# Six-layer windowed attention: interleaved token order with one value transfer per chunk, second norm and one Newton step on ScalarE

## The chip, the cores and the metric

The kernel runs on one core of a Trainium2 chip. The metric is device time in microseconds (us): the median of three executions before the change is 3436.73 us (3434.03 to 3436.86). The engines are TensorE (PE in the profile, with its weight loads as PEld), VectorE (DVE), ScalarE (ACT), GpSimd (POOL), and SyncE (SP), which here only issues DMA transfers. "ns" is nanoseconds.

## The reference

The input x has 32 sequences of 128 tokens and 128 channels, all in float32. Two blocks follow each other.

1. A cross-attention over a context of the same size (16 heads of 8 channels, 4 key/value heads, a time bias), added to x. The change touches none of its arithmetic.
2. Six layers, each an attention and a feed-forward part. Cut to what matters:

```python
for i in range(6):
    x = attn_layer(shift_tokens(x), Wqkv[i], q_scale[i], k_scale[i], Wo[i]) + x
    x = ffn_layer(shift_tokens(x), ln_g[i], ln_b[i], W1[i], b1[i], W2[i], b2[i]) + x

# attn_layer: 16 heads of 64 channels, windows of 32 tokens
q, k, v = split(x @ Wqkv)                 # per head
q, k = l2norm(q) * q_scale, l2norm(k) * k_scale
q, k = rotary(q) * scale, rotary(k) / scale
out = local_attention(q, k, v)            # a window sees itself and the window before it
return out @ Wo
# ffn_layer: layernorm, then a * gelu(gate), then W2
```

A sequence of 128 tokens is four windows of 32. A query in window u sees the keys of windows u-1 and u, under a mask.

## The kernel before, in words

**Work and stages.** The 32 sequences are 8 groups of 4 (`GB`). After the cross-attention (the first 430 us or so) each of the 6 layers goes over the 8 groups, and each group over its 4 sequences. One sequence of one layer is called a unit here: there are 6 x 32 = 192. The feed-forward part works on a whole group at once: 48 of these.

**A unit** (`unit`, L770) works on the transposed tokens of its group, `xh` and `xl` (the high and the low part, so that three fast matmuls give a product exact enough; `split3`, L433):

- `qk` (L435 to L437, four chunks c): tokens times weights for q and k, into a PSUM bank, token on the partition. `sq` (L787, ACT) squares it, `tab` (L793, DVE) multiplies it with the rotary tables, `ss` (L816, DVE) sums the squares, `add` (L809, POOL) adds the two rotary parts.
- `newton` (L383) turns the 32 sums per token into 1/sqrt: a floor (L396, DVE), Ln and Exp (L399, L402, ACT), then one Newton step y*(1.5 - 0.5*v*y*y) in three DVE instructions (L405, L409, L415). `mul` (L834, POOL) scales the rows, `tq` (four PE transposes a chunk, L441) turns them, `evq` (L838, ACT) copies the result from PSUM to SBUF.
- `y` (PE, L435 to L437 again, four chunks): tokens times the product of value and output weights. `yt` (L851, ACT) copies a chunk to SBUF as 128 tokens x 512. The four windows u of 32 tokens are then laid beside each other, so that a 32-partition block holds one chunk: `dm` (L861), four transfers per chunk, one per window, issued by SP; 16 per unit.

```python
for u in range(4):
    S.op("dm", lambda u=u: nc.sync.dma_start(ysh[0].t[32 * c:32 * c + 32, u * 512:(u + 1) * 512],
                                             yt.t[32 * u:32 * u + 32, :]), pri, [yt], ysh, k=c)
```

- `msk` (L884, ACT) puts the mask into two PSUM banks, `sc` (L879, PE, 64 small matmuls) adds the scores, then `mx` (L892, DVE), `fold` (L893, PE, subtracts the maximum), `ex` (L895, ACT), `sm` and `rl` (L896, L897, DVE), `pl` (L898, POOL), `pt` (L900, DVE transpose in blocks of 32).
- `av` (L913, PE, 56 matmuls over two bank halves) multiplies weights with `ysh` and needs all 16 transfers of its unit.

**A group** begins with `ax` (PE transposes of the tokens, L762), `axh` (L763, ACT copy) and `axl` (L764, DVE). It ends with `ffn` (L919): residual (L921, DVE), token shift (two DMAs on SP, L752 and L753), `st`/`ag` (L927, L931, DVE), the norm's 1/sqrt with its Newton step on POOL, `xn` (L939: four DVE instructions, 128 x 128 each, subtract mean and multiply), `ptn` (transposes, L441), `xnh`/`xnl`, `gate`/`pa` (PE, L435 to L437), `gel` (L961, ACT), `um` (L969, DVE), `w2` (L980, PE), residual (L984, DVE).

**The order of the work.** A planner in the kernel (`Sched`, L79) places every operation by a list schedule: `COST` (L32) has the engine, the occupancy and the latency that it assumes for each name, `LATER` (L55) shifts an operation's priority (in units; a number after the name is the chunk), `KEEP` (L63) keeps PSUM banks free, and the buffer pools (L247 to L286) say how many of each tile there are: 5 general PSUM banks (`pj`), 2 for scores, 3 `yt`, 2 `ysh`, 4 `qT`, 10 `rt`. The result is a fixed order of instructions on each engine and on SP's queue; the chip then runs each engine's list in order, with semaphores between them. So whatever stands first in a list and waits holds up all that stands behind it.

Of the kernel before, what the change touches and what calls it, by code (L numbers as in the profile page):

```python
# [23 lines left out]
NYD = 6  # L24
NS = 2
YD = "sb"
ADD = "pool"
XN = "dve"
# [6 lines left out]
    mxs=("POOL", .26, .30), dmx=("DVE", .17, .25), dnw=("DVE", .18, .25), ln=("ACT", .2, .24), ep=("ACT", .2, .24), nw=("POOL", .31, .34),  # L35
    mul=("POOL", 1.08, 1.1), tq=("PE", .45, .70), evq=("ACT", .5, .62), evk=("ACT", .5, .62),
    y=("PE", .69, .90), yt=("ACT", .5, .62), dm=("SP", .62, 2.3), dw=("SP", .62, 3.5), dr=("SP", .62, 4.5),
# [3 lines left out]
    eps=("POOL", .22, .26), lnf=("ACT", .22, .21), epf=("ACT", .22, .21), nwf=("POOL", .3, .34), xn=("DVE", 1.05, 1.13), xn2=("POOL", 1.08, 1.1),  # L41
# [13 lines left out]
LATER = dict(y=3, xtr=0.75, ptn=1.5, fold=0.35, qk=-0.5, xsc=-1, axh=-1, evk=-0.25, ss=0.25, sc=0.25, sq=0.5, um=0.75,  # L55
    axl=-1.5, tq=1.25, xev=1.75, mul=0.75, mx=-1, evq1=-1.0, tab0=0.25, lnb=0.5, um1=-1, xpj=0.75, yt1=-1.5, rl1=0.75,
    dw=-1, gel=0.75, xn1=1, nw=-0.25, msk0=2, yt3=-1.25, ta3=0.5, pwm=-0.4, ag=0.25, tq0=1.5, pa0=-0.5, dnw=1, io=0.6,
    xnh=1.5, ep=-1.5, mx1=0.25, pt1=1.5, adda=0.9, ex1=1, gel1=0.35, dr=-0.15, ta1=1.5, msk=-1.5, adda1=2, xo=1.5,
    ta0=0.5, sm0=2.85, xsb=3, rl0=-1, mx0=-1, wve=-1.5, um0=0.25, evq2=-1.5, tq1=0.5, add3=2.1, xnl=2, gate1=0.5,
    nwf=1, xn2=0.25, add=1.5, lof=-1.5, yt2=0.5, wvp=0.75, ta=-0.5, xn=-0.5, ldw=-0.25, tq2=-0.25, res2=0.35, pt=0.25,  # L60
    xat=2)

KEEP = dict(qk=1, y=1, gate=1, pa=3, xtr=0, xpj=0, pv=1, td=1, xsc=0, wvp=2, mp=2, bip=2, sc0=0, ax=0, tq=0)  # L63
# [159 lines left out]
def body(ctx: ExitStack, tc: tile.TileContext, x, ctx_in, fside, mask_in, xWq, xWk, xWv, xWo, xtw,  # L223
         Wqkv, q_scale, k_scale, Wo, ln_g, ln_b, W1, b1, W2, b2, cst, x1d, y2d, out):
# [18 lines left out]
    def pool(name, n, shape, dt=F32, inorder=True):  # L243
        S.pool(name, [lambda d, i=i: tl(f"{name}_{i}_", shape, d or dt) for i in range(n)], inorder)
# [7 lines left out]
    if ADD == "dma":  # L252
        pool("rt", 5, [P, 1024])
    else:
        pool("rt", 10, [P, 512])
    pool("qT", 4, [P, 512])
    pool("ysh", 2, [P, 2048])
    pool("yt", 3, [P, 512], inorder=False)
# [3 lines left out]
    pool("xl", 2, [P, GB, P], F32R)  # L262
    pool("nh", 1, [P, 512], F32R)
# [38 lines left out]

    S.pool("yd", [y2d[i] for i in range(y2d.shape[0])], False)
# [79 lines left out]
    def newton(names, pri, V, src, n, floor, eps, pool_, cols):  # L383
        v, y, t = [Buf(p) for p in pool_]

        def sl(b):
            return b.t[:, 0:n]
# [16 lines left out]
        def f3():  # L404
            e.tensor_tensor(sl(t), sl(y), sl(y), op=ALU.mult)  # L405
# [18 lines left out]
        S.op(names[3], f3, pri, [y], [t])  # L424
# [182 lines left out]
    def xgroup(g):  # L607
# [66 lines left out]
        if ADD == "dma":  # L674
            two = [Buf("rt", dt=F32R), Buf("rt", dt=F32R)]
            qs = [(two[t // 2], t % 2 * 512) for t in range(4)]
        else:
            qs = [(Buf("rt", dt=F32R), 0) for t in range(4)]
# [77 lines left out]
    def lgroup(l, g, w):  # L756
        base = l * NU + g * GB
        G = {"po": Buf("po")}
        pt = Buf("pj")
        hi, lo = G["x"] = Buf("xh"), Buf("xl")  # L760
        pri = base - 1.0
        S.op("ax", lambda: tr4(pt.t, [xsg(g)[:, k] for k in range(GB)]), pri, [X[g], XS[g]], [pt], also=[hi, lo])  # L762
        S.op("axh", lambda: nc.scalar.copy(hi.t, grp(pt.t)), pri, [pt], [hi])  # L763
        S.op("axl", lambda: nc.vector.tensor_tensor(lo.t, grp(pt.t), hi.t.bitcast(F32), op=ALU.subtract), pri, [pt, hi],  # L764
             [lo])
        for j in range(GB):
            unit(l, g, j, w, G, base + j)
        ffn(l, g, w, G, base + GB - 1)

    def unit(l, g, j, w, G, pri):  # L770
# [4 lines left out]

        hs = [(Buf("rt"), Buf("t")) for _ in range(2)] if ADD == "dma" else None

        def proj(c):
            pp, sq = Buf("pj"), Buf("sq")
            rt, t = hs[c // 2] if hs else (Buf("rt"), Buf("t"))  # L780
            o = c % 2 * 512 if hs else 0
            tok = Buf(None, 0) if hs else rt
            rts.append((rt, o, tok))
# [13 lines left out]
            def ta():  # L797
                nc.vector.tensor_tensor(rt.t[:, o:o + 512].rearrange("p (h d) -> p h d", d=64),
                                        pp.t.rearrange("p (h d) -> p h d", d=64), bc(tab.t[:, c // 2, 0], 8), op=ALU.mult)

            def tb():
                nc.vector.tensor_tensor(
                    t.t[:, o:o + 512].rearrange("p (h s d) -> p h s d", s=2, d=32)[:, :, ::-1, :],
                    pp.t.rearrange("p (h s d) -> p h s d", s=2, d=32),
                    bc(tab.t[:, c // 2, 1].rearrange("p (s d) -> p s d", s=2), 8), op=ALU.mult)

# [4 lines left out]
            if hs:  # L811
                S.op("ta", ta, pri, [pp, tab], [rt], also=[t], k=c)
                S.op("ta", tb, pri, [pp, tab], [t], k=c)
            else:
                S.op("tab", tab2, pri, [pp, tab], [t], k=c)
            S.op("ss", lambda: nc.vector.tensor_reduce(ss.t[:, c * 8:(c + 1) * 8], sq.t.rearrange("p (h d) -> p h d", d=64),  # L816
                                                       axis=AX.X, op=ALU.add), pri, [sq], [ss], k=c)
            if not hs:
                S.op("add", add, pri, [t], [rt], k=c)
            elif c % 2:  # L820
                S.op("adda", lambda: nc.gpsimd.dma_start(rt.t, t.t, accum_op=ALU.add), pri, [t, rt],
                     [rt, *(x[2] for x in rts[-2:])], k=c)
# [4 lines left out]
        for c in range(4):  # L827
            def tr(c):
                (rt, o, tok), pt, d = rts[c], Buf("pj"), Buf("qT")
                qT.append(d)  # L830

                def mul():
                    rv = rt.t[:, o:o + 512].rearrange("p (h d) -> p h d", d=64)
                    nc.gpsimd.tensor_tensor(rv, rv, rn.t[:, c * 8:(c + 1) * 8].unsqueeze(2).to_broadcast([P, 8, 64]),  # L834
                                            op=ALU.mult)
                S.op("mul", mul, pri, [tok, rn], [tok], also=[rt], k=c)
                S.op("tq", lambda: tr4(pt.t, [rt.t[:, o + k * P:o + (k + 1) * P] for k in range(4)]), pri, [tok], [pt], also=[rt, d], k=c)
                S.op("evq", lambda: nc.scalar.copy(d.t, pt.t), pri, [pt], [d], k=c)  # L838
            tr(c)
# [3 lines left out]
        yds = [Buf("yd"), Buf("yd")]  # L843
        for c in range(4):
            def yy(c):
                py, yt = Buf("pj"), Buf("yt")
                mh, ml = w["m"][c]
                yd = yds[c // 2]
                S.op("y", lambda: split3(py.t, (xh.t[:, j, :], xl.t[:, j, :]), (mh.t, ml.t)), pri, [xh, xl, mh, ml], [py],
                     also=ysh, k=c)  # L850
                S.op("yt", lambda: nc.scalar.copy(yt.t, py.t), pri, [py], [yt], k=c)  # L851
                if YD == "dram":
                    S.op("dw", lambda: nc.sync.dma_start(yd.t[:, c % 2], yt.t), pri, [yt], [yd], k=c)
                    if c % 2:
                        r = slice(32 * c - 32, 32 * c + 32)
                        S.op("dr", lambda: nc.sync.dma_start(
                            ysh[0].t[r].rearrange("p (u n) -> p u n", u=4),
                            yd.t.rearrange("u c i n -> (c i) u n")), pri, [yd], ysh, k=c)
                else:
                    for u in range(4):  # L860
                        S.op("dm", lambda u=u: nc.sync.dma_start(ysh[0].t[32 * c:32 * c + 32, u * 512:(u + 1) * 512],  # L861
                                                                 yt.t[32 * u:32 * u + 32, :]), pri, [yt], ysh, k=c)
            yy(c)
# [55 lines left out]
    def ffn(l, g, w, G, pri):  # L919
# [15 lines left out]

        if XN == "dve":
            def xnf():
                for k in range(GB):
                    nc.vector.tensor_scalar(xn.t[:, k * P:(k + 1) * P], xsg(g)[:, k], mv.t[:, k, 0:1], r.t[:, k:k + 1],  # L939
                                            op0=ALU.subtract, op1=ALU.mult)  # L940
            S.op("xn", xnf, pri, [X[g], XS[g], mv, r], [xn])
        else:
            S.op("xn1", lambda: nc.gpsimd.tensor_tensor(grp(xn.t), xsg(g), mv.t[:, :, 0:1].to_broadcast([P, GB, P]),
                                                        op=ALU.subtract), pri, [X[g], XS[g], mv], [xn])
            S.op("xn2", lambda: nc.gpsimd.tensor_tensor(grp(xn.t), grp(xn.t), r.t[:, 0:GB].unsqueeze(2).to_broadcast([P, GB, P]),
                                                        op=ALU.mult), pri, [xn, r], [xn])
# [64 lines left out]
def _constants():  # L1011
# [15 lines left out]
    rot = np.concatenate([QK_SCALE * cos * scale, QK_SCALE * sin * scale * sgn, cos / scale, sin / scale * sgn], 1)  # L1027
    idn = np.eye(N)
# [37 lines left out]
```

## Time and profile before

| | before |
|---|---|
| median of three executions | 3436.73 us |
| the profiled execution | 3450.15 us |
| its span (first to last instruction) | 3448.4 us |
| granted TensorE clock, mean | 0.972 |
| `dm` issues on SP (L861) | 3072, median 589 ns, 507 to 2076 ns |
| a `dm` from issue to landing | 1.9 / 2.0 / 4.0 us (min / median / max) |
| `xn` on DVE (L939) | 192 instructions, 131 us busy |
| first Newton product on DVE (L405) | 192 instructions, 79 us busy |
| `evq` on ACT (L838) | 768 instructions, 426 us busy |

The page has six parts: busy time of each engine; the span in 40 slices; DMA queues; the chain of work that ended last (followed back from the last instruction, at each step to what released it); the costliest groups of instructions; and DMA issues with their time to landing. A busy PE is not a PE at its peak, since the ends of pipelined matmuls are modelled. The view of waits lists who was idle and what ended it; the view of a line lists its instructions, what they waited for and who waited for them; the view of windows sums busy time over stretches of the span.

### The profile page before, as it was taken

How to read it: one execution, taken by the hardware profiler on the slowest of the kernel's cores; microseconds unless marked ns; L12 is line 12 of the kernel's file. 1: busy time of each engine (PE TensorE's matmuls, PEld its weight loads, DVE VectorE, ACT ScalarE, POOL GpSimd, SP SyncE). 2: the span in 40 equal slices, each digit the busy share in tenths (PEclk: the TensorE clock that was granted, in tenths of full speed). 3: DMA queues.
4: the chain of work that ended last, by engine and by line, in shares of the span. 5: the costliest groups of instructions: out<-in, count | busy, mean ns of one | idle time of the engine just before them, and what ended most of it. 6: DMA issues, size and time to landing. Idle time of an engine off the chain costs nothing.

```text
span 3448.4 us, 118846 instructions
## 1 busy us (share of the span) xinstructions
PE 3113.7 (90%) x47887; PEld 2404.7 (70%) x47887; DVE 2917.7 (85%) x6115; ACT 2227.7 (65%) x4415; POOL 2413.6 (70%) x2470
## 2 busy tenths in 40 slices
PE   8877899898799999799999999999999999999997
PEld 5554677676576777577777777777777777777775
DVE  5556998889678998779999889998899988899984
ACT  6766666666466666566766666666666667676664
POOL 6546877677557777656777767777677777677773
PEclk9998999999899999899999999999999999999998
DMA  4200132323133333233233333332332333333332
GB/s 105 58 13 10 48 78 67 76 68 90 41 87 74 74 80 76 56 92 74 69 79 79 87 77 78 75 82 68 91 80 69 79 74 85 79 75 87 82 78 71
DMA packets 253765, 251.06 MB, mean 73 GB/s; under 512 B 127486, under 2 KB 148258, under 8 KB 253218
## 3 DMA queue, kind: packets, MB, share of 16 engines
q1 hardware_dynamic: 252786, 243.12, 28.8%
q8 instruction: 380, 6.23, 0.9%
q14 instruction: 167, 1.37, 0.1%
q10 hardware_dynamic: 432, 0.34, 0.0%
HBM read 25.24 MB, written 4.19 MB: 9 GB/s over the span
## 4 chain that ended last, share of the span: by engine, by line
PE 34%; DVE 26%; DMA 11%; SPq 11%; ACT 10%; issue 6%; POOL 2%; ACTq 0%; POOLq 0%; DVEq 0%
SPq L861 10%; PE bank__68 L913 7%; DMA xt<-xt 2%; PE bank__66 L879 2%; PE bank__64 L441 1%; PE bank__67 L879 1%; PE bank__63 L441 1%; PE bank__61 L441 1%; PE bank__65 L441 1%; PE bank__63 L435 1%; PE bank__62 L435 1%; PE bank__62 L441 1%; PE bank__65 L435 1%; PE bank__61 L435 1%; PE bank__63 L436 1%
## 5 line engine op out<-in xcount | busy, mean ns | idle before, releaser
L884 ACT COPY bank__66<-mask 128x512 f32<-128x512 f32 x192 | 117.0, 610 | 5.7 <-PE bank__66 L362 4.4
L884 ACT COPY bank__67<-mask 128x512 f32<-128x512 f32 x192 | 116.5, 607 | 1.5 <-PE bank__67 L362 1.1
L724 ACT ACTIVATE ysh__88<-ysh__88 128x512 f32<-128x512 f32 x96 | 60.7, 634 | 57.0 <-POOL ysh__88 L722 56.9
L961 ACT ACT_TABLE_LOAD x48 | 61.6, 1283 | 0.9
L241 ACT ACT_TABLE_LOAD x48 | 61.6, 1283 | 0.9
L921 DVE TENSOR_TENSOR xt<-bank__68,xt 128x512 f32<-128x512 f32 x48 | 33.0, 687 | 16.7 <-PE bank__68 L913 16.5
L441 PE MATMUL bank__61<-cs,ysh__88 128*128 128x128 f32 x84 | 15.5, 315 | 10.2 <-ACT ysh__88 L724 10.2
L441 PE MATMUL bank__63<-cs,ysh__88 128*128 128x128 f32 x80 | 14.6, 312 | 10.8 <-ACT ysh__88 L724 10.5
L441 PEld LDWEIGHTS bank__63<-cs,ysh__88 128*128 128x128 f32 x80 | 9.9, 156 | 15.0 <-ACT ysh__88 L724 12.8
L441 PEld LDWEIGHTS bank__61<-cs,ysh__88 128*128 128x128 f32 x84 | 10.9, 160 | 13.6 <-ACT ysh__88 L724 12.2
L441 PE MATMUL bank__62<-cs,ysh__88 128*128 128x128 f32 x76 | 14.5, 324 | 5.6 <-ACT ysh__88 L724 5.4
L441 PE MATMUL bank__64<-cs,ysh__88 128*128 128x128 f32 x68 | 12.7, 318 | 7.6 <-ACT ysh__88 L724 7.5
L441 PE MATMUL bank__65<-cs,ysh__88 128*128 128x128 f32 x76 | 13.3, 302 | 6.4 <-ACT ysh__88 L724 6.1
L441 PEld LDWEIGHTS bank__62<-cs,ysh__88 128*128 128x128 f32 x76 | 10.7, 168 | 8.4 <-ACT ysh__88 L724 7.6
L695 DVE TENSOR_TENSOR xt<-bank__68,xt 128x512 f32<-128x512 f32 x8 | 5.5, 685 | 12.8 <-PE bank__68 L693 12.8
L441 PEld LDWEIGHTS bank__64<-cs,ysh__88 128*128 128x128 f32 x68 | 8.6, 159 | 10.9 <-ACT ysh__88 L724 10.2
L441 PEld LDWEIGHTS bank__65<-cs,ysh__88 128*128 128x128 f32 x76 | 9.5, 154 | 9.5 <-ACT ysh__88 L724 8.7
L991 POOL TENSOR_TENSOR raw__50988<-raw__50988,xt 128x512 f32<-128x512 f32 x1 | 1.3, 1262 | 19.7 <-DVE xt L984 19.7
L718 DVE CUSTOM_DVE_ANT_0 ysh__88<-bank__63,rt__2156 128x128 f32<-128x128 f32 x12 | 2.8, 287 | 12.7 <-ACT S__90 L727 6.2
L727 ACT COPY ysh__88<-bank__63 128x512 f32<-128x512 f32 x20 | 11.9, 597 | 1.8 <-PE bank__63 L441 1.6
L727 ACT COPY ysh__88<-bank__61 128x512 f32<-128x512 f32 x21 | 12.3, 586 | 1.2 <-PE bank__61 L441 1.1
L718 DVE CUSTOM_DVE_ANT_0 ysh__88<-bank__61,rt__2550 128x128 f32<-128x128 f32 x12 | 2.8, 288 | 12.1 <-ACT S__90 L727 5.6
(24588 smaller groups left out, 15904.7 us busy)
## 6 DMA issues: line engine op xcount, KB each, us to landing
xt<-xt SPq DMA_DIRECT2D x96, 112.0 KB, 2.5
xt<-in_x SPq DMA_DIRECT2D x16, 128.0 KB, 3.2
x_scratch<-xt SPq DMA_DIRECT2D x8, 256.0 KB, 3.0
xt<-xt SPq DMA_DIRECT2D x96, 15.0 KB, 2.2
stg__750<-in_L_ffn_Wo SPq DMA_DIRECT2D x1, 512.0 KB
stg__1904<-in_L_ffn_Wo SPq DMA_DIRECT2D x1, 512.0 KB
stg__20461<-in_L_ffn_Wo SPq DMA_DIRECT2D x1, 512.0 KB
stg__28190<-in_L_ffn_Wo SPq DMA_DIRECT2D x1, 512.0 KB
```

Source lines behind the costliest of these rows:

```text
L241: S.back = lambda: nc.scalar.preload_act_table_set("natural_log_exp_and_others")
L435: nc.tensor.matmul(pt, lh, rh, start=True, stop=False)
L436: nc.tensor.matmul(pt, lh, rl, start=False, stop=False)
L441: nc.tensor.transpose(dst[:, k * P:(k + 1) * P], srcs[k], ident)
L724: S.op("xex", lambda: nc.scalar.activation(sm.t, sm.t, AF.Exp), pri, [sm], [sm], table="E")
L727: S.op("xev", lambda: nc.scalar.copy(sm.t, pt.t), pri, [pt, sm], [sm])
L861: S.op("dm", lambda u=u: nc.sync.dma_start(ysh[0].t[32 * c:32 * c + 32, u * 512:(u + 1) * 512], yt.t[32 * u:32 * u + 32, :]), pri, [yt], y ...
L879: nc.tensor.matmul(s4[a][32 * c:32 * c + 32, half, wd, lo:64], q[r, c * P + 32 * wd:c * P + 32 * wd + 32], k[r, c * P + 32 * wd - 32 + lo: ...
L884: S.op("msk", lambda b=b: nc.scalar.copy(b.t, mask), pri, (), [b], k=a)
L913: nc.tensor.matmul(po.t[32 * wd:32 * wd + 32, j * P:(j + 1) * P], p5[a][:, half, wd, blk, :], ysh[0].t[:, u * 512 + h * P:u * 512 + (h + 1 ...
L921: S.op("res", lambda: nc.vector.tensor_tensor(xv(g), hv(po.t), xv(g), op=ALU.add), pri, [po, X[g]], [X[g]])
L961: S.op("gel", lambda: nc.scalar.activation(u.t[0:n], pg.t[0:n], AF.Gelu, bias=b1c.t[0:n, 1, i:i + 1]), pri, [pg, b1c], [u], table="G", k=i)
```

## The change

Four things are changed together.

1. **Token order.** `axh` and `axl` write the transposed tokens so that token u*32 + i stands at place 4*i + u. All products (q, k and values) then come out with that token on partition 4*i + u. The rotary tables are put in the same order on the host. `evq` puts q and k back in plain order: it reads PSUM at a step of four elements and writes SBUF in a row.
2. **Values.** A chunk of 128 partitions x 512 now lies in the order of the target's 32 partitions x 2048, and one `dm` per chunk takes the place of four. `dm` has a new assumed latency (3.2 for 2.3).
3. **Second norm.** `xn` moves from DVE to ACT: four activations with scale and bias per partition. A small DVE instruction, `nmr`, first makes the bias, -mean/sqrt. `ysq` (ACT Square) takes the place of the first of the three DVE instructions of the Newton step of the q and k norms.
4. **The planner's numbers.** `LATER` is replaced whole, `KEEP` has `pa=1` for 3 and no `ax`, and the assumed costs of the Newton steps rise (`dmx` .17 to .32, `dnw` .18 to .30). Every engine's list therefore stands in another order. Code for branches not in use is removed, and the memory of `yt` is allocated after `xl`.

```diff
-    S.op("axh", lambda: nc.scalar.copy(hi.t, grp(pt.t)), pri, [pt], [hi])
-    S.op("axl", lambda: nc.vector.tensor_tensor(lo.t, grp(pt.t), hi.t.bitcast(F32), op=ALU.subtract), pri, [pt, hi],
-         [lo])
+    def woven(a):
+        return a.rearrange("p b (i u) -> p b u i", u=4)
+    def plain():
+        return pt.t.rearrange("p (b u i) -> p b u i", b=GB, u=4)
+    S.op("axh", lambda: nc.scalar.copy(woven(hi.t), plain()), pri, [pt], [hi])
+    S.op("axl", lambda: nc.vector.tensor_tensor(woven(lo.t), plain(), woven(hi.t.bitcast(F32)), op=ALU.subtract), pri,
+         [pt, hi], [lo])
...
-                S.op("evq", lambda: nc.scalar.copy(d.t, pt.t), pri, [pt], [d], k=c)
+                S.op("evq", lambda: nc.scalar.copy(d.t.rearrange("p (k u i) -> p k u i", k=4, u=4),
+                                                   pt.t.rearrange("p (k i u) -> p k u i", k=4, u=4)), pri, [pt], [d], k=c)
...
-                    for u in range(4):
-                        S.op("dm", lambda u=u: nc.sync.dma_start(ysh[0].t[32 * c:32 * c + 32, u * 512:(u + 1) * 512],
-                                                                 yt.t[32 * u:32 * u + 32, :]), pri, [yt], ysh, k=c)
+            S.op("dm", lambda: nc.sync.dma_start(ysh[0].t[32 * c:32 * c + 32, :], yt.t), pri, [yt], ysh, k=c)
...
-            e.tensor_tensor(sl(t), sl(y), sl(y), op=ALU.mult)
+            if small:
+                nc.scalar.activation(sl(t), sl(y), AF.Square)
+            else:
+                e.tensor_tensor(sl(t), sl(y), sl(y), op=ALU.mult)
...
-                for k in range(GB):
-                    nc.vector.tensor_scalar(xn.t[:, k * P:(k + 1) * P], xsg(g)[:, k], mv.t[:, k, 0:1], r.t[:, k:k + 1],
-                                            op0=ALU.subtract, op1=ALU.mult)
+        S.op("nmr", lambda: nc.vector.scalar_tensor_tensor(mv.t[:, :, 0], mv.t[:, :, 0], -1.0, r.t[:, 0:GB], op0=ALU.mult, op1=ALU.mult),
+             pri, [mv, r], [mv])
+        def xnf():
+            for k in range(GB):
+                nc.scalar.activation(xn.t[:, k * P:(k + 1) * P], xsg(g)[:, k], AF.Identity, bias=mv.t[:, k, 0:1],
+                                     scale=r.t[:, k:k + 1])
...
+    rot = rot.reshape(4, 32, 4 * D).transpose(1, 0, 2).reshape(N, 4 * D)
...
-    dm=("SP", .62, 2.3)   dmx=("DVE", .17, .25)   dnw=("DVE", .18, .25)   xn=("DVE", 1.05, 1.13)
+    dm=("SP", .62, 3.2)   dmx=("DVE", .32, .40)   dnw=("DVE", .30, .38)   xn=("ACT", .92, 1.0)   nmr=("DVE", .2, .28)   ysq=("ACT", .2, .24)
-LATER = dict(y=3, xtr=0.75, ptn=1.5, fold=0.35, qk=-0.5, ...)
-KEEP = dict(qk=1, y=1, gate=1, pa=3, ..., sc0=0, ax=0, tq=0)
+LATER = dict(y=3.25, xtr=-0.25, ptn=3, fold=0.75, qk=-0.5, ..., av=-0.5, ...)
+KEEP = dict(qk=1, y=1, gate=1, pa=1, ..., sc0=0, tq=0)
```

## The prediction, before the changed kernel was run

> **What bounds the kernel now.** I read the page's first and fourth part, then the windows of the layer stage, then the waits, then SP's own timeline.
>
> ```profile
> ## 1 busy us (share of the span) xinstructions
> PE 3113.7 (90%) x47887; PEld 2404.7 (70%) x47887; DVE 2917.7 (85%) x6115; ACT 2227.7 (65%) x4415; POOL 2413.6 (70%) x2470
> ...
> ## 4 chain that ended last, share of the span: by engine, by line
> PE 34%; DVE 26%; DMA 11%; SPq 11%; ACT 10%; issue 6%; POOL 2%; ACTq 0%; POOLq 0%; DVEq 0%
> ```
>
> PE and DVE are both nearly full, and yet 22% of the chain is DMA transfers and SP's issuing. The layer stage alone, by windows:
>
> ```profile
> core 0: us, PE busy (x) PEld busy (x) DVE busy (x) ACT busy (x) POOL busy (x), PEclk, DMA share, GB/s
> 430.00:3400.00 2970.00, 2727.57 (x44540) 2142.29 (x44541) 2620.65 (x4641) 1935.12 (x3833) 2138.68 (x2123) 0.98 0.32 77
> ```
>
> In it lie 185 units (so many first Newton products, L405), so a unit takes 2970/185 = 16.05 us, with PE busy 14.74, DVE 14.17, POOL 11.6, ACT 10.5. PE's work is the same after the change, so what can be gained here is its idle 242 us, 1.31 a unit, and little more (the modelled ends of its matmuls hide some short waits).
>
> Summed over the buffers, PE with its loads is idle 237 us: 58 before `fold`, which waits for `mx` (DVE, L892); 47 before `av` (23 put down to the transfers into `ysh`, 24 to nothing that the profile names); 24 before `tq`, for `mul`; 22 before `ptn`, for `xn` (DVE, L939); some 30 for ACT's copies and squares; 56 in small posts. The transfers are next:
>
> ```profile
> 2217.08 2.41 SPq L861 DMA_DIRECT2D ysh__33152<-yt__33172  x4
> 2219.59 3.00 SPq L861 DMA_DIRECT2D ysh__33152<-yt__33179  x4
> 2222.68 2.44 SPq L861 DMA_DIRECT2D ysh__33152<-yt__33203  x4
> 2225.22 3.43 SPq L861 DMA_DIRECT2D ysh__33152<-yt__33307  x4
> ```
>
> Second column: how long four issues take. SP goes from one chunk to the next without a pause and needs about 12 us of the 16 for one unit. And in the chain of waits:
>
> ```profile
> 1535.02 0.60 SPq L861
> 1535.62 0.04 issue
> 1535.66 0.59 SPq L861
> 1536.25 0.04 issue
> 1536.30 3.23 DMA ysh__21919<-yt__21947
> 1539.53 0.02 issue
> 1539.55 0.04 ACTq L851
> 1539.59 0.04 issue
> 1539.63 0.04 ACT yt__22125 L851
> ```
>
> The transfer that reads a `yt` buffer must land before ACT may fill the buffer again, and ACT then does nothing else, since its list is in order. Over the stage ACT stands idle 206 us in 190 such waits before L851, and DVE then waits 100 us for ACT's squares (L787).
>
> **Part 1: one transfer for four.** 3072 issues of mean 656 ns are 2014 us of SP; 768 issues remain. Nearest rows for one: L696, also 256 KB, 366 ns; L753 mean 949 ns; I take L752's 672, so 516 us, 2.7 us a unit for 10.5. A chunk's way today, from the end of `yt`: median 2.5 us until SP comes to it, 2.9 for four issues, 1.4 more until the last lands (2.0 from issue) = 6.8. After: up to 0.5 for SP, then one landing of 256 KB. Bounds: 2.0 (the 64 KB landing) and 4.9 (the chain above: its round of issues begins at 1534.65 us, the landing is at 1539.53). I take 3.0, the median of L696, which moves as many bytes (2.3 to 3.7). So 3.3 for 6.8, and most of ACT's 206 us go.
>
> But the cover goes too. Between a unit's last `y` and its `av` the old order of PE has work of 8.6 us (median; per operation 0.69 for `y`, `qk`, `gate`, `pa`, 0.44 for four transposes, 1.5 for `sc`, 2.0 for `av`, 0.23 for `fold`, 0.17 for a `w2`, from the starts of one to the next in the trace), the new order 4.7. Needed are 0.2 (end of `y`), 0.6 (`yt`), 3.3 and some 0.2 of semaphores: 4.3. So `av` stays as tight as it is: of the 47 us I keep 40.
>
> **Part 2: DVE.** `xn` leaves with 131 us of busy time and the first Newton product with 79; `nmr` comes, 48 times. The neighbours of its kind (L409, L415) have means of 0.31 and 0.33 us, so 15 us (bounds 0.13 to 1.25 each, 6 to 60). Net -195 us, 1.0 a unit: DVE 14.2 to 13.2. These instructions are so dear because they vary: L939 from 305 to 1476 ns, L405 from 130 to 1305, for equal shapes.
>
> **Part 3: ACT.** `ysq`: 192 times 0.245 (L399, also 128x32) = 47 us. `xn`: the nearest row is L661, four 128x128 activations with one operand per partition, 0.36 us each, one every 0.27, so 1.2 us for four; a second operand adds up to 0.1 each (L631 691 ns, a plain copy 595), so 1.2 to 1.6; I take 1.4, 67 us. ACT 10.5 to 11.1 us a unit: under PE, DVE and POOL, and in place of the waits that go. On `ptn`'s path 1.4 us and one more hop through DVE (`nmr`, 0.3 and its queue) replace four instructions of mean 0.74 (3 us): of 22 us I keep 10.
>
> [...]
>
> **Part 4: the order of the tokens.** `evq` reads PSUM at a step of 16 bytes, 768 times; ACT, now 606 ns. No row of ACT has such a read. The element time is (606-245)/(512-32) = 0.75 ns. The one strided PSUM read is DVE's L744: 16 elements 128 bytes apart in 250 ns, against 186 for 8 elements from SBUF (L897): the 64 ns more are at most 4 ns for each strided element, and nothing if they are PSUM's. Ends: 0, and 512 x 4 ns = 2 us per `evq`, which is far out in rival 3; I take 0, since a PSUM read of 128 elements in short runs (L745, DVE) takes 285, hardly more than the 16 strided ones. `axh` and `axl` write at the same step, 48 times each: 0 to one doubling, 0 to 62 us off PE's path; I take 0. A gain has no reason in either.
>
> [...] If each element cost twice, the estimate is 0.38 us more per `evq`, and no run here shows it yet.
>
> **Part 5: the order of the work.** `fold` stands 1.6 us of PE work behind `sc` (median) for 2.1: less cover, but DVE's queue before `mx` is shorter by 7%. I keep 45 of 58. `tq`: `mul` waits for a Newton step that loses one DVE queue; 14 of 24. ACT's posts: 10 of 30, since it is no longer held by `yt`. Small posts: 40 of 56. The cross-attention and the tail also stand in a new order; nothing in a page tells the sign: 0, with 15 us either way.
>
> **Sum.** Kept: 40 + 10 + 45 + 14 + 10 + 40 = 159 of 237, so -78 over 185 units, -81 over 192. Waits hidden in PE's modelled busy time (start to start, `av` alone exceeds its usual step by 87 us behind transfers, 40 more than the idle time shows): -30. Total about -110. The profiled execution took 3450.15 us, its span 3448.4; the median is 13 lower. 3450 - 110 = 3340 in a profile; 3437 - 110 = 3327, which I round to **3325 us**.
>
> **Rivals.**
>
> 1. *Faster, and by far more.* The transfers are 22% of the chain, not 47 us; when the loop yt - SP - landing - yt breaks, all lists close up and PE idles only the 0.4 us a unit that its best groups show (1.3 us in the 61 from one residual, L921, to the next at 2564 us). For it: SP's timeline. Against: PE is full to 92% in that stage. -0.9 x 192 = -175: 3260.
> 2. *The gain is eaten at `av`.* The new order leaves 4.7 us where 4.3 are needed. If a 256 KB transfer lands at 3.7 (L696's maximum), every `av` waits 0.4 us more, 77 us, and with ACT's lateness the whole 110 are gone: 3437.
> 3. *Slower: the strided `evq`.* It stands between `tq` and `sc`, with 1.4 us of PE work between (median) and 0.9 needed. It decides from about +0.6 us per `evq` (2.6 times the element time), where ACT's 11.1 + 4 x 0.6 = 13.5 us a unit pass DVE's 13.2. At three times the element time, +0.77: ACT 11.1 + 4 x 0.77 = 14.2 us a unit, as full as DVE is now, `sc` waits 0.3 and more each time, 58 us, and ACT's squares and copies come late to DVE: about one DVE-like share of idle back (-110 gone) and 58 to 100 on top: 3520. For it: no row of ACT shows such a read. Against: L744 beside L745.
> 4. *The new lists are simply worse on the chip*, since each engine waits at its head: nothing in the rows prices it; it is the spread below.
>
> **Numbers.** Forecast (3280 to 3415) 0.50; rival 1 (below 3280) 0.20; rival 2 with rival 4 within 0.2% (3430 to 3444) 0.06, and between 3415 and 3430 0.03; above 3444, rival 3 0.12 and rivals 2 and 4 0.09. Faster by over 0.2% 0.73, within 0.2% (what a measurement of this kernel can hardly tell from no change) 0.06, slower 0.21. The range leaves out the lower third of rival 1 and the upper half of what is slower: 3225 to 3480.
>
> **What would show it.** Right: SP's L861 (now one line per chunk) at 768 issues with gaps between, landing near 3.0 us; ACT's idle time before `yt` for transfers under 60 us; DVE busy near 2720, ACT near 2340; `evq` at 606 ns; PE busy the same with 130 to 170 us idle in the stage. Wrong: `evq` above 0.9 us; a landing above 3.7 us and `av` idle above 47 us; `xn` on ACT above 2 us for four; PE idle above 240 us in spite of shorter transfers, which would make it the order.

## The result, and the profile after

The changed kernel takes 3693.04 us (median of 4 executions, 3687.03 to 3703.99); the kernel before, beside it on the same chip, 3436.52 us. The ratio is 1.0752, 95% interval 1.0721 to 1.0782: 7.5% slower. The forecast was 3325 us, and the range ended at 3480.

The profiled execution took 3703.99 us, its span 3702.2, at a mean granted TensorE clock of 0.942 (0.972 before). The page's first and fourth part, in answer to those of before:

```profile
PE 3116.5 (84%) x47887; PEld 2455.9 (66%) x47887; DVE 2789.7 (75%) x5779; ACT 2337.5 (63%) x4799; POOL 2414.8 (65%) x2470
...
## 4 chain that ended last, share of the span: by engine, by line
PE 44%; DMA 29%; ACT 10%; DVE 8%; issue 6%; POOL 1%; SPq 0%; ACTq 0%; POOLq 0%; DVEq 0%
```

The instructions became what the change wanted: DVE fell by 128 us, ACT is at 2337, SP's issuing has gone from the chain (11% before, 0% now). But DMA rose from 11% to 29% of the chain. The layer stage by windows:

```profile
430.00:3650.00 3220.00, 2720.26 (x44354) 2183.35 (x44353) 2484.08 (x4289) 2034.65 (x4190) 2129.75 (x2110) 0.95 0.47 71
```

The last three numbers are the clock, the mean busy share of the DMA engines and GB/s. The share was 0.32 before and is 0.47 now, for no more bytes per second (77, now 71). The third part of the page says the same for SP's transfers over the whole span:

```profile
q1 hardware_dynamic: 215922, 242.97, 42.5%
```

That is packets, MB and share; before it was 28.8% for 243.12 MB. In the trace a packet of 2048 bytes takes 140 ns before (median) and 232 ns after. So the transfers are fewer and each is much slower. SP's own list around one unit (start, duration of the issue), and then the chain of waits in the same stretch:

```profile
1831.78 0.55 SPq L828 DMA_DIRECT2D ysh__24349<-yt__24396  x1
...
1837.03 0.61 SPq L828 DMA_DIRECT2D ysh__24349<-yt__24490  x1
1837.74 0.59 SPq L828 DMA_DIRECT2D ysh__24349<-yt__24498  x1
1838.49 0.55 SPq L828 DMA_DIRECT2D ysh__24349<-yt__24513  x1
```

```profile
1837.99 0.47 ACT yt__24513 L827
...
1838.49 6.74 DMA ysh__24349<-yt__24513
1845.23 0.14 issue
1845.36 3.48 PE bank__68 L880 x56
```

SP takes each chunk at once, 0.03 us after the copy (median; 2.5 before). Then the last chunk needs 6.74 us to land, since the two issued just ahead of it are still on their way (the first one's packets had ended at 1834.3 us), and `av` (now L880) can only start then. The view of L828 gives who waited, and the time to landing, which it knows for 98 of the 768 transfers:

```profile
who waited for it (us, times):
  PE bank__68 L880: 328.5, 159
  PEld bank__68 L880: 115.9, 50
...
DMA to landing us min/median/max: 3.8/5.3/7.8
```

Summed over the stage (430 us to the tail), PE with its loads is idle 493 us, of which 335 before `av`: 1.75 us a unit. Before it was 237, with 47 before `av`. So `av` adds 288 us, all other waits together give back 32, and 256 is what the span grew by (254).

The 5.3 us have two parts. A chunk that follows the one before it by 5 us or more lands after 4.2 us (median of 19 of the 98 known landings), one that follows within 0.8 us after 5.7 (24 of them). So the single transfer is slow, and the chunks of a unit hold each other up besides.

### The profile page after: what moved, and what is told of

Its sections match the earlier page's. It is cut to its first block, busy times and chain, and to the rows that moved or that the text cites. A ratio compares the mean times of both kernels' runs of the same rounds, so it can differ in the third digit from the quotient of the medians.

```text
span 3702.2 us, 115231 instructions
## 1 busy us (share of the span) xinstructions
PE 3116.5 (84%) x47887; PEld 2455.9 (66%) x47887; DVE 2789.7 (75%) x5779; ACT 2337.5 (63%) x4799; POOL 2414.8 (65%) x2470
## 4 chain that ended last, share of the span: by engine, by line
PE 44%; DMA 29%; ACT 10%; DVE 8%; issue 6%; POOL 1%; SPq 0%; ACTq 0%; POOLq 0%; DVEq 0%
PE bank__68 L880 12%; PE bank__66 L846 2%; PE bank__67 L846 2%; PE bank__63 L429 1%; PE bank__61 L429 1%; PE bank__62 L429 1%; PE bank__64 L429 1%; PE bank__65 L429 1%; PE bank__63 L431 1%; PE bank__63 L430 1%; PE bank__62 L435 1%; PE bank__62 L431 1%; PE bank__62 L430 1%; PE bank__61 L431 1%; PE bank__61 L430 1%
## 5 line engine op out<-in xcount | busy, mean ns | idle before, releaser
L888 DVE TENSOR_TENSOR xt<-bank__68,xt 128x512 f32<-128x512 f32 x48 | 33.0, 687 | 76.6 <-PE bank__68 L880 76.5
L685 DVE TENSOR_TENSOR xt<-bank__68,xt 128x512 f32<-128x512 f32 x8 | 5.5, 685 | 19.6 <-PE bank__68 L683 19.6
L948 DVE TENSOR_TENSOR xt<-bank__62,xt 128x512 f32<-128x512 f32 x10 | 6.8, 684 | 8.9 <-PE bank__62 L944 8.9
L948 DVE TENSOR_TENSOR xt<-bank__61,xt 128x512 f32<-128x512 f32 x10 | 6.8, 684 | 7.7 <-PE bank__61 L944 7.5
```

Source lines behind the costliest of these rows:

```text
L888: S.op("res", lambda: nc.vector.tensor_tensor(xv(g), hv(po.t), xv(g), op=ALU.add), pri, [po, X[g]], [X[g]])
```

## The experiments

In all of them "packet" is the median time of the 2048-byte packets in the trace, and "in bursts" their bytes over the time in which at least one of them was under way. PE's idle time is that of PE and PEld together from 430 us to the tail.

### Is it the landing, the order of the lists, or ScalarE's part?

**wide_dst**: each chunk's transfer writes 128 partitions.

```diff
-nc.sync.dma_start(ysh[0].t[32 * c:32 * c + 32, :], yt.t)
+nc.sync.dma_start(ysh[0].t[:, 512 * c:512 * c + 512], yt.t)
```

> The changed kernel with one edit: each chunk's transfer writes 128 partitions x 512 instead of 32 partitions x 2048. The same 256 KB, the same lists on every engine; the values land in other places, so the attention output is another one. Theory A: a 256 KB transfer into 32 partitions is held to some 128 GB/s by its destination (2 KB packets take 232 ns in the median against 140 before), lands after 5.3 us instead of the 3.0 forecast, and the new lists leave only 4.7 us of PE work between a unit's last y and its av. Then here packets fall to 140 to 160 ns, the landing to 3.0 to 3.6 us, PE's idle time before av from 335 us to under 100, and the time to 3380 to 3480. Theory B (the new lists are worse in themselves): about 3690, with the idle time elsewhere. Theory C (it is the size or the source of one transfer, not its destination): landing stays near 5.3 us and the time near 3690.

Measured: 3221.40 us, ratio 0.9375 (0.9355 to 0.9394); packets 84 ns. Its queue, and L828's waiters:

```profile
q1 hardware_dynamic: 215922, 242.97, 21.9%
```

```profile
who waited for it (us, times):
  PEld bank__68 L880: 5.1, 10
...
  PE bank__68 L880: 2.2, 5
...
DMA to landing us min/median/max: 2.2/2.3/4.5
```

The same packets and bytes take half of the DMA engines' time, the landing falls to 2.3 us (2.3 behind a long pause and 2.4 right behind another chunk), and the waits of PE and PEld for it, added up, from 444 us to 7. The time goes from 7.5% above the kernel before to 6.3% below. That is further than theory A expected (140 to 160 ns, 3.0 to 3.6 us, 3380 to 3480 us): it had the cause right and the size too small. Only the place of the values in the target differs, partitions and length of the rows (which of the two, dst_spread tells below): neither the new lists nor ScalarE's part nor the steps of the copies is what costs.

**four_new_lists**: the changed kernel with the chunk's transfer cut in four by window (source `yt.t[u::4, :]`).

> The changed kernel with its chunk's transfer cut into four again, one per window (32 partitions at a step of 4, 64 KB each), all lists as in the changed kernel. Theory A: SP needs 2.5 us for a chunk again, and the chunks of a unit stand close together (3.4 us of PE work from y0 to y3), so the last lands some 6.8 us after its yt; over the 4.7 us of cover that is 3.1 us of waiting per unit where the changed kernel has 1.75: 3850 to 4000. Theory C (one large transfer is what is slow): faster than the changed kernel, 3450 to 3600.

Measured: 3974.60 us, ratio 1.1563 (1.1532 to 1.1594), as theory A expected. Packets take 82 ns, so the pieces are fast; but SP's issuing is back in the chain, in lists that leave it no time:

```profile
PE 42%; ACT 17%; DMA 15%; SPq 11%; DVE 7%; issue 6%; POOL 1%; ACTq 0%; POOLq 0%; DVEq 0%
```

**one_old_lists**: the lists of before, with the interleaved tokens and one transfer at the place of the first of four.

> The kernel before with the new token order and one transfer per chunk, issued where the first of the four stood; the lists of PE, DVE, ACT and POOL are those of before, second norm and Newton step stay on DVE. Theory A: the old lists leave 8.6 us of PE work between the last y and av; needed are 0.2 + 0.6 + 0.1 + 5.3 + 0.2 = 6.4 us, less than the 7.8 of the four transfers. So PE waits less before av than before: 3390 to 3440, though axh and axl are 0.5 us dearer, 48 times each. Theory C' (the slow transfer costs by itself, wherever it stands): 3600 or more.

Measured: 3408.11 us, ratio 0.9921 (0.9905 to 0.9938). The packets are as slow (220 ns) as in the changed kernel, and it is faster than before all the same: the old order has 8.6 us of work between the last `y` and `av`, the new one 4.7.

**act_old_later**: the kernel before with the second norm, `nmr` and `ysq` on ScalarE, re-planned with the old `LATER`.

> The kernel before with only the second norm (xn, nmr) and the Newton step's square on ACT: plain token order, four transfers, old priorities, the lists planned anew with these operations' assumed costs. The prediction's own terms: DVE -195 us, ACT +111 us, ptn's path 12 us better; PE waits less for xn and mx: 3370 to 3420. Rival (moving work off DVE buys nothing, since PE waits for SP and the transfers, and a plan made anew is as likely worse): 3430 to 3500.

Measured: 3383.20 us, ratio 0.9838 (0.9809 to 0.9866); PE idle 199 us for 237. ScalarE's part, planned anew, is a gain by itself.

**woven_old_lists**: the kernel before with the token order alone (four transfers, source `yt.t[u::4, :]`).

> The kernel before with the interleaved order of the tokens alone: its lists, its four transfers per chunk (now from every fourth partition), its second norm and Newton step on VectorE; the tables permuted, the copies with steps. What the order of the tokens costs by itself: axh and axl take 0.5 us more in 48 pairs, 48 us beside TensorE's work; evq as before; packets 82 ns for 140. My sum from the traces: 0 to +30 us, 3430 to 3470 us. If the read at a step delayed the scores (the prediction's third rival), above 3500 us; if the quicker packets alone count, 3400 us or below.

Measured: 3436.46 us beside 3426.54, ratio 1.0027 (1.0014 to 1.0040). The order costs 10 us, although its packets take 82 ns for 140; that nothing is gained by them fits SP's issuing as the pace of four transfers.

**one_act_old**: all four parts on the old priorities.

> The old priorities with all four parts of the change in the instructions: interleaved tokens, one transfer per chunk at the place of the first of four, second norm and first Newton product on ScalarE. The parts so far, each by itself on the old priorities: one transfer 3408 for 3437 us, ScalarE's part 3383, token order alone +10. If they add, 3340 to 3375 us. If ScalarE's part shortens the cover before the value product, the slow landing shows again: above 3400 us.

Measured: 3306.05 us, ratio 0.9611 (0.9585 to 0.9638), some 50 us more gain than the product of one_old_lists and act_old_later (0.9760, 3355 us). The worry that the slow landing would show again fell: PE and PEld wait 25 us for the transfers. Where the 50 us come from was not traced.

**plan_occ** and **plan_54**: the changed kernel, with only the planner's number for the transfer changed.

```diff
-dm=("SP", .62, 3.2)
+dm=("SP", 2.1, 4.6)    # plan_occ
+dm=("SP", .62, 5.4)    # plan_54
```

> The changed kernel with one number of the planner changed: a value transfer is assumed to hold its queue for 2.1 us and to land after 4.6 us (0.62 and 3.2 in the changed kernel), as measured. Same instructions, another order. Theory A (the 256 KB transfer lands in 5.3 us where the order leaves 4.7 us of cover): the planner now puts more work between the values and their use; TensorE's idle time before the value product falls from 335 us to under 150 and the time to 3300 to 3480 us. Rival B (the new shifts of priority are bad in themselves, or were fitted to the old number): the idle time moves elsewhere, and the time stays above 3600 us.

> The changed kernel with the planner's latency of a value transfer at 5.4 us in place of 3.2 and its hold of the queue left at 0.62 (plan_occ had 4.6 and 2.1, and took 3293 us). It tells whether the latency or the queueing of four chunks has to be known. If the latency is enough: 3270 to 3350 us. If the planner has to know that chunks queue behind each other (the last of four lands later than 5.4 us after its copy): more idle time before the value product than in plan_occ, 3330 to 3480 us.

Measured: plan_occ 3292.69 us, ratio 0.9584 (0.9564 to 0.9604), a little better than its 3300 to 3480; plan_54 3360.48, ratio 0.9770 (0.9738 to 0.9802). plan_occ's chain, by engine, and then the waiters of L828:

```profile
PE 45%; DVE 24%; ACT 13%; issue 7%; DMA 6%; POOL 3%; POOLq 0%; ACTq 0%; DVEq 0%; SPq 0%
```

```profile
  PE bank__68 L880: 27.2, 33
  PEld bank__68 L880: 8.2, 5
```

The transfers are still slow (219 ns a packet, 45.3% of the DMA engines), yet PE and PEld wait 35 us for them and not 444, and DMA is 6% of the chain: the last copy of a unit ends 6.3 us ahead of `av` (median) with other work between, where the changed kernel's 5.6 us end in waiting. The instructions are as many and of the same kinds as in the changed kernel; only their order differs, and PE's idle time falls from 493 us to 202, before `av` from 335 to 31. It also gives a version with the reference's output that beats both kernels, by 4.2% and 10.8%. plan_54 tells that the latency alone is not the whole number: PE and PEld wait 58 us for the transfers there (35 in plan_occ). That fits chunks that queue behind each other, but it is a third of the 68 us between the two runs; the rest was not traced.

### Why is the landing slow?

In the changed kernel the first 80 packets or so of a lone chunk take 84 ns, all within 0.45 us; of the other 48 most take 200 to 330 ns (medians by place over the 92 chunks whose packets run alone). Why the pace changes there no run shows. The following runs change only from and to which partitions a chunk goes, by which queue, and in the last four in two transfers for one. The edits, in place of the transfer of the changed kernel (`src` is `yt.t`, `D` is `ysh[0].t`):

```python
dst64:         D[64*(c//2):64*(c//2)+64, 1024*(c%2):1024*(c%2)+1024] <- src
dst_spread:    D[c::4, :] <- src
dst_half:      D[64*(c//2)+c%2 : 64*(c//2)+64 : 2, :] <- src
dst_cross:     D[(48, 80, 16)[c] : +32, :] <- src;  c = 3: D[0:16] <- src[0:64], D[112:128] <- src[64:128]
two_queues:    as changed; odd chunks issued by ScalarE behind its copy
halves_queues: the same with the chunks in the order 0, 2, 1, 3, so that SyncE issues 0, 1 and ScalarE 2, 3
straight64:    D[s:s+64, 512*c:+512] <- src[s:s+64],      s = 0, 64
cross64:       D[64-s:128-s, 512*c:+512] <- src[s:s+64],  s = 0, 64
even64:        D[s::2, 512*c:+512] <- src[s::2],          s = 0, 1
step8:         D[2*c+s::8, :] <- src[s::2],               s = 0, 1
```

> The changed kernel, but each chunk's transfer writes 64 partitions x 1024 (rows of 4 KB) for 32 x 2048 (rows of 8 KB); the values so lie elsewhere and the output is not the reference's. In the changed kernel a 2048-byte packet takes 232 ns and a transfer lands in 5.3 us; writing 128 partitions it was 84 ns and 2.3 us, at 3221 us. Theory P (the pace is set by how many neighbouring partitions are written at a time): twice as many, so about half the packet time (110 to 150 ns), landing 3.3 to 3.9 us, and the time between the two, 3300 to 3500 us. Theory R (long rows are what is slow): rows of half the length, so also faster, and by the same step; dst_spread tells the two apart. If neither holds, 230 ns and 3690 us stay.

> The changed kernel, but each chunk's transfer writes 32 partitions that stand four apart (c, c+4, c+8, ...) with rows of 8 KB as before, not 32 neighbours; the values lie on other partitions and the output is not the reference's. Bytes, packets, rows and issues are those of the changed kernel. Theory P (neighbouring partitions share a way in): packets near 84 ns, landing 2.3 to 2.8 us, time as with 128 partitions, 3210 to 3300 us. Theory R (32 rows of 8 KB are slow wherever they are): 232 ns, 5.3 us, 3690 us.

> The changed kernel, with chunks 1 and 3 of a unit issued by ScalarE right behind its copy and only chunks 0 and 2 by SyncE, so that two transfers to different blocks of 32 partitions can run side by side. Theory P (a block of 32 neighbouring partitions takes in so much and no more): two blocks take twice as much; packets stay slow each but the four transfers of a unit land about 2 us earlier, and the time falls to 3400 to 3560 us, less some 0.1 us of ScalarE per issue (40 us in all). If the 16 DMA engines are the limit whatever they write to, nothing is gained: 3690 us, or more by ScalarE's 384 issues.

> The changed kernel, but each chunk's transfer writes every second partition of one half of the 128 (64 partitions, 32 rows of 8 KB); the values lie elsewhere and the output is not the reference's. Measured so far: 32 neighbours 232 ns a packet and 3693 us, 64 neighbours 220 ns and 3641 us, 32 partitions over all 128 84 ns and 3213 us. Theory H (each half of 64 partitions takes in at most the 135 GB/s that bursts show, wherever in it the rows lie): 215 to 235 ns, landing 5.3 us, 3620 to 3720 us. Theory N (rows that are direct neighbours disturb each other): every second partition is enough to be faster, below 180 ns and 3500 us.

> The changed kernel, but the blocks of 32 neighbours are moved by 16 partitions: chunk 0 writes partitions 48 to 79, chunk 1 80 to 111, chunk 2 16 to 47, chunk 3 goes as two transfers of half the bytes to 0 to 15 and 112 to 127 (one more issue a unit); the values lie elsewhere and the output is not the reference's. Theory H (a limit for each half of 64): chunk 0 is now written to both halves, 16 rows each, and chunk 1 and 2, one behind the other, to different halves; so chunk 0's packets are near 84 to 130 ns while 1 and 2 stay above 180, and the time is somewhere between 3400 and 3620 us. Theory N (neighbouring rows disturb each other): nothing changes, 230 ns for all, 3690 us.

> The kernel two_queues (3720 us) with the chunks taken in the order 0, 2, 1, 3: SyncE issues chunks 0 and 1 (lower half of the partitions), ScalarE chunks 2 and 3 (upper half). The same instructions at the same places, the same bytes; only which half each queue writes differs. Theory H (135 GB/s for each half, the two halves side by side): the two queues no longer meet in one half, bursts reach well above 135 GB/s, packets 85 to 150 ns, the last landing 2 to 3 us earlier: 3250 to 3420 us. Theory N or a limit of the DMA engines themselves: as two_queues, 3720 us.

> The changed kernel, but each chunk goes as two transfers of 64 partitions x 512: partitions 0 to 63 of the copy to 0 to 63 of the target and 64 to 127 to 64 to 127, each packet to the partition that it comes from; the values lie elsewhere and the output is not the reference's, and SyncE has 8 issues a unit for 4. Theory X (what is written to partitions far from those that are read goes over one shared way of about 135 GB/s; to the same partitions it does not): packets near 84 ns, landing of each under 2.6 us, 3200 to 3320 us. Theory D (64 or fewer neighbours at a time take in no more than 135 GB/s, whatever they are read from): packets above 140 ns in bursts and above 3450 us.

> The kernel straight64 with the halves exchanged: partitions 0 to 63 of the copy are written to 64 to 127 and the other way round. Bytes, packets, issues and the number of partitions written are those of straight64; only each packet's way is another. The output is not the reference's. Theory X (the shared way): packets 180 to 240 ns, 135 GB/s in bursts, 3550 to 3750 us. Theory D: the same as straight64, within 1%.

> The kernel straight64 (two transfers a chunk of 64 partitions x 512, to the partitions that they come from; 3274 us, 148 ns a packet), but one of them takes the even and the other the odd partitions. As many partitions, bytes and issues; the output is not the reference's. [...] If the number of partitions in a transfer sets the pace: 148 ns and 3274 us as before.

> The changed kernel with two transfers a chunk, each from 64 alternate partitions to 16 rows of 8 KB that stand eight apart over all 128; the values lie elsewhere and the output is not the reference's. Span theory (what matters is that the rows are spread over all 128, as in dst_spread with 84 ns and 3213 us): 84 to 100 ns, below 3300 us. [...]

| run | written by one transfer | packet, ns | in bursts, GB/s | us | ratio to before (95%) |
|---|---|---|---|---|---|
| changed kernel | 32 neighbours | 232 | 135 | 3693.04 | 1.0752 (1.0721 to 1.0782) |
| dst64 | 64 neighbours | 220 | 136 | 3641.01 | 1.0591 (1.0561 to 1.0621) |
| dst_half | every second of 64 | 220 | 136 | 3687.77 | 1.0755 (1.0731 to 1.0779) |
| dst_cross | 32 neighbours, 16 further on | 236 | 134 | 3749.65 | 1.0942 (1.0914 to 1.0970) |
| two_queues | 32 neighbours, 2 queues | 225 | 136 | 3719.77 | 1.0838 (1.0812 to 1.0863) |
| halves_queues | the same, a queue for each half | 225 | 137 | 3708.92 | 1.0822 (1.0797 to 1.0848) |
| dst_spread | 32 over all 128 | 84 | 268 | 3212.61 | 0.9355 (0.9335 to 0.9376) |
| wide_dst | 128 | 84 | 270 | 3221.40 | 0.9375 (0.9355 to 0.9394) |
| straight64 | 64 neighbours (read: the same 64) | 148 | 176 | 3273.93 | 0.9526 (0.9495 to 0.9558) |
| cross64 | 64 neighbours (read: the other 64) | 148 | 176 | 3274.95 | 0.9526 (0.9497 to 0.9555) |
| even64 | every second of 128 (read: the same) | 84 | 225 | 3264.76 | 0.9531 (0.9507 to 0.9554) |
| step8 | 16, eight apart (read: every second) | 84, mean 112 | 179 | 3292.35 | 0.9613 (0.9592 to 0.9634) |

What follows, one theory after the other:

- *A limit by the number of neighbours* (theory P) fell with dst64: twice as many gained 5% in packet time, not half. That the rows are long (theory R) fell with dst_spread, which has the same 32 rows of 8 KB.
- *A limit for each half* (theory H) fell with dst_cross and halves_queues: two queues that write to different halves move no more than two that write to the same one (137 and 136 GB/s; 143 in both while packets of both queues were under way, 236 and 248 us). dst_half, which it had right, also told against theory N (direct neighbours). An issue takes 0.555 us on ScalarE in these two runs; the 0.1 in the expectation of two_queues was an assumption that no run shows (ScalarE's three issues in the kernel before take 0.40 to 0.45 us). dst_cross (3750 us) lies above what either theory expected; its one more issue a unit was not traced.
- *A shared way between far partitions* (theory X) fell with cross64: it is straight64 to 0.03%.
- *Theory D* (64 or fewer neighbours take in no more than 135 GB/s) had straight64's packets right (148 ns) and its time wrong (above 3450 us forecast, 3274 measured).
- *The number of partitions, or their spread over all 128?* even64 beside straight64 shows that it is not the count: 64 partitions at 84 ns and at 148. step8's time (3292 us) and its median packet (84 ns) are those of the span theory, its mean packet (112 ns) is above it.

The last four rows need care. Their transfers have 64 packets, fewer than the 80 or so that went at 84 ns above, and the packets of the next one start 0.64 to 0.67 us later: 128 KB in that time are some 200 GB/s, so it is the issuing that paces them, and their GB/s are no limit of the target. In straight64 and cross64 two transfers in turn write different halves, besides. Their slow packets are there from the start, and packet for packet as in the kernel before, which also reads neighbours, 32 of them (medians of the first four: 111, 147, 160 and 156 ns in all three). woven_old_lists writes the same 32 neighbours as the kernel before and reads every fourth partition: 82 ns for 140. So reading neighbours costs too, by itself and at once, where writing them costs after some 80 packets. straight64, cross64 and even64 change both sides together; by their pattern the loss is in the reading. step8 reads as even64 does, so its slow packets, some 28 of 64 at the start of a transfer (108 to 181 ns), come from what it writes.

So this is shown: the pace is set by which partitions one transfer writes (232 ns a packet into 32 neighbours, 84 into 32 spread over all 128, dst_spread) and, by woven_old_lists, reads (82 ns from every fourth partition, 140 from 32 neighbours); not by their number (64 at 84 ns in even64, at 148 in straight64), the rows (8 KB in dst_spread too) or the queue (225 ns in two_queues and halves_queues), nor, in transfers of 128 KB, by the distance between source and target (148 ns in straight64 and cross64). What makes one set of partitions quick and another slow no run shows, and it stays open why step8 is slow only at the start of a transfer. A kernel with the reference's output whose one transfer per chunk goes at 84 ns a packet was not found: `av` needs chunk c on partitions 32c to 32c + 31.

## Why the prediction was wrong

**The step that failed** is in part 1: "I take 3.0, the median of L696, which moves as many bytes (2.3 to 3.7)". Measured are 5.3 us (3.8 to 7.8), above the upper of the bounds given (2.0 and 4.9). L696 moves as many bytes, but out of 128 partitions to a scratch in DRAM, in packets of 512 bytes; `dm` writes 32 partitions in packets of 2048. The nearest row by bytes was not the nearest by target. Its "median" is also the middle of only two known landings, 2.3 and 3.7 us. And the sum priced one transfer alone: by itself a chunk lands after 4.2 us, inside the bounds, and the rest up to 5.7 is the queueing behind the unit's other chunks, for which the sum had no term. The sign that was named in advance, a landing above 3.7 us and `av` idle above 47, is the one that came.

**What it did.** Part 1 needed 0.2 + 0.6 + 3.3 + 0.2 = 4.3 us against 4.7 of cover. With 5.3 in place of 3.0 it is 6.6, so 1.9 us a unit are missing, 365 us over 192 units; 335 us of idle time stand before `av`. "So `av` stays as tight as it is" was the wrong conclusion from the right comparison: the place had 0.4 us of slack, and the whole loss came out there. Rival 2 had the place and the mechanism ("The gain is eaten at `av`"), with 3.7 us as its worst landing: 0.4 us missing. (By the sum in part 1 that landing leaves 0.3 us missing, 4.3 + 0.7 - 4.7, or 58 us for the 77.) At 5.3 the sum gives 1.9 x 192 = 365 us, less the 110 gained elsewhere: +255, where the profile has +254. That this fits so well is luck: `av` added 288 us, and PE's other waits gave back 32. Rival 2 had no more than its share of 0.06, 0.03 and 0.09, since its worst case was another row's maximum.

**The other steps:**

- SP: 768 issues of 0.55 us (I took 0.67), at once behind the copy. ACT's waits for transfers before `yt` fell from 206 us to 118 only, not under 60, for the same slow landing (17 us in wide_dst).
- Part 2: DVE fell by 128 us, not 195. `nmr` takes 0.44 us (0.31 taken), 21 us in all, and `axl` costs 21 more. The other 40 us are spread over unchanged instructions: the floor of the Newton step 83 us for 72, `ss` 499 for 491, `sm` 253 for 245, and smaller ones.
- Part 3: ACT at 2337.5 (2340 expected). The total fits by luck, since its parts do not: `ysq` takes 45 us (47 taken), the four activations of an `xn` 1.65 us, 79 in all (1.4 and 67 taken; the upper bound of 1.6 was nearer), and `axh` 24 us (0 taken). The idle time in which `ptn` waits for `xn` fell from 22 to 5 us; 10 were kept. act_old_later prices the part by itself: -55 us. An `xn` instruction takes 489 ns on ACT, where DVE took 305 at its best but 742 in the mean, and the kernel gained 1.6%.
- Part 4: `evq` 603 ns for 606, so the strided read costs nothing, and rival 3 has no case. `axh` and `axl` rose from 611 to 1114 and from 676 to 1115 ns: I took 0 within bounds of 0 to 62 us, and it is 24 and 21.
- Part 5: the idle time in which `fold` waits for `mx` fell from 58 to 12 us; 45 were kept. Part of that is only that PE now stands before `av` instead: in wide_dst 32 us stand before `fold`.
- Rival 1 (3260) and rival 4 (the lists are simply worse): wide_dst settles both. With a landing of 2.3 us the new lists take 3221 us, below rival 1's 3260; so they are good lists where the transfer is quick.

So the forecast had the mechanism right, and the term that decided, the landing, was mis-sized: 5.3 us for 3.0. The rest of the sum was too small the other way: with a quick landing the change gains 217 us (wide_dst), where 110 were forecast. The range was too narrow since the upper bound for an unseen transfer was taken from rows that write somewhere else.

## What to carry to other kernels

One transfer for four saves issues, but its landing has to be priced by the partitions that it reads and writes, not by its bytes (256 KB landed after 5.3 us into 32 neighbours, after 2.3 over all 128): compare packet times of a row with the same target, look in the trace at how full the DMA engines are, and add what the transfers issued just before it still have to do. Where a planner sets the order, a changed operation needs its measured hold and latency, with the queueing behind its neighbours: the same instructions took 3693 us with 3.2 us in the table and 3293 with 2.1 and 4.6. And where a step keeps a wait "as tight as it is", its price is a slope: one unit of error there times the number of units is the width that the range needs.

## What the runs showed of the hardware that was not expected

- A 2048-byte packet between two places in SBUF takes 82 to 84 ns, 140 to 148 or 219 to 236 in the median, by the partitions that its transfer reads and writes (above, run by run).
- About 80 packets of a lone chunk of the changed kernel go at 84 ns before the slowing starts, so transfers of 64 KB (32 packets) do not show it: four_new_lists writes the same 32 neighbours at 82 ns. Its transfers also come some 0.63 us apart, which is no more than 104 GB/s. Reading 32 neighbours shows from the first packets (140 ns in the kernel before; the first four 111, 147, 160 and 156).
- Writing SBUF at a step of 16 bytes makes a 128x512 copy of ACT slower by 0.50 us (`axh`), and a subtraction of DVE that also reads one operand so by 0.44 us (`axl`); reading PSUM at that step costs ACT nothing (603 ns for 606).
- PE's busy time for 47887 instructions is 3113.7 us in the kernel before at a mean granted clock of 0.972, 3116.5 in the changed kernel at 0.942, and 2990.5 in dst_spread at 0.982. So removing waits took time out of the busy part too (126 us between the last two), and the mean clock alone does not order the three; the cause is open.
